# Propagations of two batches as seven block products, the layer norms' last step on ScalarE, and seven groups in flight, in a four-layer graph network

## The chip, the cores and the metric

The kernel runs on one core of a Trainium2 chip. Four engines compute: TensorE (PE, matrix products into PSUM; PEld is its loading of weights), VectorE (DVE), ScalarE (ACT) and GpSimd (POOL). SyncE (SP) issues the DMAs. Each engine works through its own queue in order; between engines there are semaphores. The metric is the device time of one execution in microseconds; lower is better. All numbers are float32.

## What is computed

x has 64 batches of 256 nodes with 128 features, adj is a 256x256 matrix. Four layers follow each other, each of them `x = layernorm(x + layer(x))`. A propagation is `adj @ x` for every batch.

```python
# layer 0: powers 1 to 3 of adj, the same adj twice, seven weights
parts = [x[..., None], chebyshev(adj, x, 3), chebyshev(adj, x, 3)]
y = einsum('bnik,iok->bno', concatenate(parts, axis=3), weight_1)
# layer 1
y = einsum('nm,bmo->bno', adj, einsum('bnf,fo->bno', x, weight)) + bias
# layer 2: normalised adjacency
A_norm = d[:, None] * (adj + eye) * d[None, :]
y = einsum('bnc,oc->bno', einsum('nm,bmc->bnc', A_norm, x), W) + b
# layer 3: five gated steps
m = einsum('nm,bmd->bnd', adj, h)
av = concatenate([m, m], axis=-1)
u3 = h @ u3_w.T + u3_b
z = sigmoid(av @ w3_w.T + w3_b + u3)
r = sigmoid(av @ w4_w.T + w4_b + u3)
hv = tanh(av @ w5_w.T + w5_b + (r * h @ u5_w.T + u5_b))
h = (1 - z) * h + z * hv
...
def layernorm(x, eps=1e-5):
    return (x - mean(x)) / sqrt(var(x) + eps)
```

## The kernel before

The 64 batches are cut into groups (line 644): 31 pairs and, at the end, two single batches (`ONES`, line 22). A group's tile has 128 partitions and 512 columns: two batches times two halves of the 256 nodes (T = 2) times 128 features. 256 nodes are therefore two 128-row blocks, and adj, held transposed in `aT`, is two by two blocks of 128x128. `a2T` is its square, `anT` the normalised matrix of layer 2, and `aTp` (lines 284 to 290) is `aT` with its rows spread for the layout that the steps of layer 3 use.

Group.record (line 532) writes down all work of one group. For layer 0: `transposes` or a transpose through DRAM (`tx`, `dx`, `xT`), the propagation `q` with `a2T`, products `first` and `second` (lines 564 and 577) into two banks `py`, and copies of these into `s0` by VectorE (line 583). Layers 1 and 2 (line 591): GpSimd adds the bias (`biased`, line 595), then come a propagation, a product with the weights and `residual`. Layer 3: five steps of a propagation `mg`, the gates `r`, `z`, `hv` on ScalarE (`gate_`), the products `pr` and `ph` with `w4T`, `w34T`, `w5T`, `u3T`, `u5T`, and on VectorE `rh`, `d`, `e` and `hT` (`tensor`, line 529). Between steps `packed` (line 500) turns the state on VectorE (`th`) and sends it through DRAM and back (`dh`, `h`); features of the two halves lie interleaved there, so that `pair_of` (line 370) reads every second element.

A propagation (line 457) is four products: for each of two batches, two halves kt as stationary operand (`lhsT`) against 256 columns of the matrix, added up in one PSUM bank `pm`. ScalarE copies the whole bank to `m` (`copied`, line 417).

A layer norm is `statistics` (line 422) and `normalise` (line 446). VectorE takes four bn_stats, four bn_aggr and an addition of eps (`ve`); GpSimd raises it to the power -0.5 (`rs`, line 438); VectorE then makes `y = (s - mean) * rs`, one tensor_scalar for each of four 128-column tiles (line 451).

No order is written by hand. Every operation is recorded with an engine, a cost, a lag and a rank in a Plan (line 50). Plan.order takes the engines' operations as they become ready in the plan's own time, the earliest start first and then the lowest rank, which is the oldest group; it gives out buffer slots of each kind (`slots`, line 199) on the way. The result is a fixed order for every engine's queue. At most `ACTIVE` = 6 groups are in flight: the first operation of a group waits in the plan for the last of the sixth before it (`gate`, line 652). In the last `LEVEL` = 6 groups the rank goes by progress, so that they end together. The last `END` = 8 batches turn the state back with TensorE (`pth`, line 640) and not through DRAM.

Of the kernel before, what the change touches and what calls it, by code (L numbers as in the profile page):

```python
# [8 lines left out]
F32 = mybir.dt.float32  # L9
# [4 lines left out]
P = 128  # L14
NB = 2
ACTIVE = 6
HEAD = 4
LEVEL = 6
# [3 lines left out]
ONES = (0, 2)  # L22
# [4 lines left out]
class Val:  # L27
# [3 lines left out]
    def __init__(self, kind, shape, name, nb=NB):  # L31
        self.kind, self.shape, self.name, self.nb = kind, shape, name, nb
        self.writer, self.readers, self.users = None, [], []
        self.slot = self.tile = None
# [15 lines left out]
class Plan:  # L50
# [9 lines left out]
    def add(self, engine, cost, lag, rank, run, reads=(), writes=(), after=()):  # L60
        if engine == "SP":
            lag += 700
        op = Op(len(self.ops), rank, engine, cost, lag, run, [*reads, *writes])
        op.deps.update(after)
        for v in reads:
            op.deps.add(v.writer)
            v.readers.append(op)
        for v in writes:
            if v.writer is not None:
                op.deps.add(v.writer)  # L70
            op.deps.update(v.readers)
            v.writer, v.readers = op, []
# [81 lines left out]
def kernel(  # L154
# [42 lines left out]
    SHAPES = {"bank": [P, 512], "x": [P, 512], "w": [P, 512], "st": [P, Q * 6], "mv": [P, Q * 2],  # L197
              "ve": [P, Q], "rs": [P, Q]}
    slots = {"bank": BANKS, "x": ACTIVE + 3, "w": 54, "dram1": 8, "dram2": 16, "st": 8, "mv": 8, "ve": 8, "rs": 8}
# [15 lines left out]
    def load(rank, name, shape, src):  # L215
        v = constant(name, shape)
# [20 lines left out]
    a_nat = load(-9, "a_nat", [P, T, N], adj.rearrange("(t p) m -> p t m", p=P))  # L237
# [55 lines left out]
    ahat, anT = constant("ahat", [P, T, N]), constant("anT", [P, T, N])  # L293
# [24 lines left out]


    w1s = load(1.3, "w1s", [P, C], w1)  # L320
    b1s = load(1.4, "b1s", [P, C], bass.AP(tensor=b1.tensor, offset=b1.offset, ap=[[0, P], [1, C]]))
    raw = {name: load(1.5, f"raw_{name}", [P, src.shape[1]], src)
           for name, src in (("w2", w2), ("w4", w4_w), ("w3", w3_w), ("w5", w5_w), ("u3", u3_w), ("u5", u5_w))}
    b2s = load(1.5, "b2s", [P, C], bass.AP(tensor=b2.tensor, offset=b2.offset, ap=[[0, P], [1, C]]))
    both = {name: constant(f"both_{name}", [P, C]) for name in ("w4", "w3", "w5", "w34")}
# [41 lines left out]
    def tile_of(v, q):  # L367
        return nat(v)[:, q, :]

    def pair_of(v, q):  # L370
        return v.ap.rearrange("p (b c t) -> p b t c", c=C, t=T)[:, q // T, q % T, :]
# [8 lines left out]
    class Group:  # L380
# [19 lines left out]
        def add(self, engine, cost, lag, run, reads=(), writes=()):  # L400
            after = () if self.first else self.gate
            self.count += 1
            op = plan.add(engine, cost, lag, self.rank(), run, reads, writes, after)
# [4 lines left out]
        def pe(self, cost, run, reads, writes):  # L408
            return self.add("PE", cost, 260, run, reads, writes)

        def dve(self, run, reads, writes, cost=None):
            return self.add("DVE", cost or dve_cost(self.width), 260, run, reads, writes)

        def act(self, run, reads, writes, cost=None):
            return self.add("ACT", cost or act_cost(self.width), 130, run, reads, writes)
# [6 lines left out]
        def statistics(self, tag, s):  # L422
            st, mv, ve, rs = (self.val(k, k + tag) for k in ("st", "mv", "ve", "rs"))
# [5 lines left out]
            def aggr():  # L429
                for q in range(self.q):  # L430
                    nc.vector.bn_aggr(mv.ap[:, 2 * q:2 * q + 2], st.ap[:, q * 6:(q + 1) * 6])  # L431
                nc.vector.tensor_scalar(ve.ap, mv.ap.rearrange("p (q k) -> p q k", k=2)[:, :, 1], EPS,  # L432
                                        None, op0=OP.add)

            self.dve(stats, [s], [st], 195 * self.q)
            self.dve(aggr, [st], [mv, ve], 67 * self.q + 142)
            self.add("POOL", 1010, 100,
                     lambda: nc.gpsimd.tensor_tensor(rs.ap, ve.ap, half[:, :self.q], op=OP.pow), [ve], [rs])  # L438
# [7 lines left out]
        def normalise(self, tag, s, mv, rs):  # L446
            y = self.val("w", "y" + tag)

            def run():
                for q in range(self.q):  # L450
                    nc.vector.tensor_scalar(nat(y)[:, q, :], nat(s)[:, q, :], mv.ap[:, 2 * q:2 * q + 1],  # L451
                                            rs.ap[:, q:q + 1], op0=OP.subtract, op1=OP.mult)

            self.dve(run, [s, mv, rs], [y], 257 * self.q)
# [245 lines left out]
```

## Time and profile before

| what | time |
|---|---|
| median of 3 runs (lowest to highest) | 1382.56 us (1382.29 to 1382.73) |
| the profiled execution | 1382.45 us |
| its span, first to last instruction | 1380.7 us |
| mean granted TensorE clock | 0.998 |
| PE: propagation products `pmg<-aTp,h` 128x256 | 1024 passes, 241.7 us |
| DVE: `y<-s,mv,rs` (line 451) | 512 instructions, 149.7 us |
| DVE: `rh<-r,hT`, 128x512 | 155 instructions, mean 725 ns |
| DVE: `s<-py` 128x256 (line 583) | 62 instructions, 25.1 us |
| ACT: `mg<-pmg`, 128x512 (line 419) | 155 instructions, mean 586 ns |
| POOL: `rs<-ve,half` (line 438) | 132 instructions, 137.9 us |
| POOL: `yb<-y,b2s` 128x512 (line 595) | 31 instructions, mean 1565 ns |

A row of the profile names line, engine, operation and the tiles that are written and read; "us" is busy time, a mean is that of one instruction. TensorE's float32 product shows as two instructions, called passes here. A busy TensorE says nothing of how fast it goes: passes overlap, and their pace is seen from the distance of their starts.

### The profile page before, as it was taken

To read this page: it belongs to the slowest core of one execution; us is meant where nothing else is said; L and a number is where in the kernel's file an instruction comes from. 1 tells how busy PE (TensorE), PEld (TensorE's weight loads), DVE (VectorE), ACT (ScalarE), POOL (GpSimd) and SP (SyncE) were. 2 spreads that over 40 slices of the span, in tenths; PEclk is the share of its full clock that TensorE was granted. 3 is DMA by queue.
4 is the path that set the end of the run, shared out by engine and by line. 5 is a ranking of instruction groups with operands and counts; after the bars stand their busy time and mean duration, and the time that the engine had idled before them with its cause. 6 is when DMAs were issued, how large, how long until landed. Compare 5 with 4: busy or idle time off the path is not lost.

```text
span 1380.7 us, 16602 instructions
## 1 busy us (share of the span) xinstructions
PE 1366.5 (99%) x5044; PEld 922.5 (67%) x5044; DVE 970.5 (70%) x2735; ACT 513.1 (37%) x833; POOL 236.1 (17%) x205
## 2 busy tenths in 40 slices
PE   9999999999999999999999999999999999999996
PEld 8866666666667766566676666667666677766664
DVE  4755686867667767776686767668685778875577
ACT  2233433333433233433424333442334332334443
POOL 1400021202111211011121211012221113210001
PEclk9999999999999999999999999999999999999999
DMA  6023233333333332343241334333232432233332
GB/s 177 31 77 91 85 115 115 91 98 105 112 107 90 109 92 75 97 137 110 64 137 54 108 108 117 95 92 106 78 107 84 118 97 85 85 92 90 86 103 65
DMA packets 271112, 134.08 MB, mean 97 GB/s; under 512 B 177584, under 2 KB 243632, under 8 KB 271024
## 3 DMA queue, kind: packets, MB, share of 16 engines
q1 hardware_dynamic: 271024, 133.03, 33.2%
q8 instruction: 40, 0.66, 0.2%
q14 instruction: 48, 0.39, 0.1%
HBM read 67.05 MB, written 65.54 MB: 96 GB/s over the span
## 4 chain that ended last, share of the span: by engine, by line
PE 97%; DVE 2%; DMA 0%; ACT 0%; issue 0%; POOL 0%; SPq 0%; POOLq 0%; DVEq 0%
PE pr L195 30%; PE ph L195 19%; PE pmg L195 19%; PE py L195 16%; PE pm L195 8%; PE pmq L195 4%; DVE y L451 1%; DMA h<-dh 0%; DVE st L427 0%; PE p_a L195 0%; PE warm L232 0%; DVE s L443 0%; DVE d L529 0%; DVE mv L431 0%; DVE e L529 0%
## 5 line engine op out<-in xcount | busy, mean ns | idle before, releaser
L195 PE MATMUL pr<-mg,w435u5T 128*128 128x512 f32 (+1 forms) x660 | 323.3, 580 | 1.7 <-ACT mg L419 1.4
L438 POOL TENSOR_TENSOR rs<-ve,half 128x4 f32<-128x4 f32 (+1 forms) x132 | 137.9, 1049 | 1049.8 <-DVE ve L432 1049.7
L529 DVE TENSOR_TENSOR d<-hv,hT 128x512 f32<-128x512 f32 (+1 forms) x165 | 113.6, 690 | 189.6 <-ACT hv L522 189.2
L195 PE MATMUL pmg<-aTp,h 128*128 128x256 f32 x1024 | 241.7, 379 | 0.4 <-DMA h<-dh 0.4
L195 PEld LDWEIGHTS pmg<-aTp,h 128*128 128x128 f32 x1024 | 200.4, 196 | 50.5 <-issue 24.4
L529 DVE TENSOR_TENSOR rh<-r,hT 128x512 f32<-128x512 f32 (+1 forms) x165 | 116.5, 706 | 128.2 <-ACT r L522 126.9
L195 PEld LDWEIGHTS pr<-mg,w435u5T 128*128 128x128 f32 x660 | 123.6, 190 | 101.0 <-issue 90.4
L419 ACT COPY mg<-pmg 128x512 f32<-128x512 f32 (+1 forms) x165 | 94.6, 573 | 257.0 <-PE pmg L195 236.5
L451 DVE TENSOR_SCALAR y<-s,mv,rs 128x128 f32<-128x128 f32 x512 | 149.7, 357 | 34.0 <-POOL rs L438 32.5
L195 PE MATMUL pr<-hT,w2u3T 128*128 128x512 f32 (+1 forms) x330 | 163.1, 580 | 1.1 <-DVE hT L529 1.1
L522 ACT ACTIVATE z<-pr,bsum 128x512 f32<-128x512 f32 (+1 forms) x165 | 111.3, 674 | 142.2 <-PE pr L195 137.4
L195 PE MATMUL ph<-mg,w435u5T 128*128 128x512 f32 (+1 forms) x330 | 163.4, 579 | 0.0
L195 PE MATMUL ph<-rh,w435u5T 128*128 128x512 f32 (+1 forms) x330 | 163.0, 579 | 0.0
L522 ACT ACTIVATE r<-pr,bsum 128x512 f32<-128x512 f32 (+1 forms) x165 | 111.3, 674 | 135.2 <-PE pr L195 132.7
L522 ACT ACTIVATE hv<-ph,bsum 128x512 f32<-128x512 f32 (+1 forms) x165 | 111.3, 674 | 53.0 <-PE ph L195 50.9
L529 DVE TENSOR_TENSOR e<-z,d 128x512 f32<-128x512 f32 (+1 forms) x165 | 113.8, 691 | 2.5
L529 DVE TENSOR_TENSOR hT<-hT,e 128x512 f32<-128x512 f32 (+1 forms) x165 | 113.1, 687 | 2.5
L427 DVE BATCH_NORM_STATS2 st<-s 128x6 f32<-128x128 f32 x512 | 109.7, 277 | 0.8
L195 PEld LDWEIGHTS ph<-rh,w435u5T 128*128 128x128 f32 x330 | 62.4, 190 | 69.3 <-issue 59.5
L195 PEld LDWEIGHTS ph<-mg,w435u5T 128*128 128x128 f32 x330 | 62.4, 190 | 67.5 <-issue 54.8
L504 DVE STREAM_TRANSPOSE th<-hT 128x512 f32<-128x512 f32 x132 | 91.0, 689 | 2.0
L195 PEld LDWEIGHTS pr<-hT,w2u3T 128*128 128x128 f32 x330 | 61.6, 190 | 42.0 <-issue 25.2
(79 smaller groups left out, 1373.7 us busy)
## 6 DMA issues: line engine op xcount, KB each, us to landing
dh<-th SPq DMA_DIRECT2D x155, 256.0 KB, 2.0
h<-dh SPq DMA_DIRECT2D x256, 128.0 KB, 2.5
x<-in_x_dram SPq DMA_DIRECT2D x31, 256.0 KB, 3.3
hT<-dh SPq DMA_DIRECT2D x124, 64.0 KB, 2.0
out_dram<-y SPq DMA_DIRECT2D x31, 256.0 KB, 2.4
xT<-dx SPq DMA_DIRECT2D x60, 128.0 KB, 2.5
dx<-tx SPq DMA_DIRECT2D x29, 256.0 KB, 2.6
dn<-tn SPq DMA_DIRECT2D x28, 256.0 KB, 2.0
```

The source lines that it names most:

```text
L195: nc.tensor.matmul(o, lhsT, rhs, start=start, stop=stop, skip_group_check=shared)
L419: self.act(lambda: nc.scalar.copy(t.ap, ps.ap), [ps], [t])
L427: nc.vector.bn_stats(st.ap[:, q * 6:(q + 1) * 6], nat(s)[:, q, :])
L438: lambda: nc.gpsimd.tensor_tensor(rs.ap, ve.ap, half[:, :self.q], op=OP.pow), [ve], [rs])
L451: nc.vector.tensor_scalar(nat(y)[:, q, :], nat(s)[:, q, :], mv.ap[:, 2 * q:2 * q + 1], rs.ap[:, q:q + 1], op0=OP.subtract, op1=OP.mult)
L504: self.dve(lambda: nc.vector.transpose(turn.ap.rearrange("p (u j t) -> p u t j", t=T, j=32), src.ap.rearrange("p (u t i) -> p u t i", t=T, ...
L522: self.act(lambda: nc.scalar.activation(t.ap, ps.ap, func, bias=bias[1], scale=1.0), [ps, bias[0]], [t], act_cost(self.width) + 100)
L529: self.dve(lambda: nc.vector.tensor_tensor(out(t), way(a), way(b), op=op), [a, b], [t])
```

## The change

A pair's propagation is a product of a 2x2 block matrix (batch by half) with the 2x2 blocks of the adjacency. It is computed with seven block products and additions around them (Strassen's scheme in Winograd's form) instead of eight. `seven` records: GpSimd makes four blocks of differences of the state's blocks in three instructions (`ts`, `tq`); TensorE multiplies in four visits (`first`, `middle`, `more`, `rest`), each product 128 columns wide, into the four 128-column parts of one bank; ScalarE keeps the first product before the second is added to it (`kept`), and later copies out the first output block; VectorE adds the others together (`post1`, `post2`) and writes `m`. Sums of the adjacency's blocks are made once on VectorE (`block_sums`). The first two groups (start below HEAD) keep the old form for `q`, since `near` is passed on as `fast=not near`; everything else, 254 propagations, takes the new one.

Further: `statistics` also makes the negated mean (`nm`) and GpSimd multiplies it with `rs`, so that `normalise` is an ACTIVATE with scale and bias on ScalarE; the copies into `s0` go to ScalarE; ACTIVE and LEVEL are 7; ONES is (0, 0), so all 32 groups are pairs. Some buffers grow, and loaded raw weights take slots instead of constants. The plan learns of several writers of one buffer (`joint`).

```diff
-ACTIVE = 6
+ACTIVE = 7
 HEAD = 4
-LEVEL = 6
+LEVEL = 7
 END = 8
 STEPS = 5
 WARM = 12
-ONES = (0, 2)
+ONES = (0, 0)
...
         for v in writes:
-            if v.writer is not None:
-                op.deps.add(v.writer)
             op.deps.update(v.readers)
-            v.writer, v.readers = op, []
+            if not joint:
+                op.deps.update(v.writers)
+                v.writers = []
+            v.writers.append(op)
+            v.readers = []
...
-    slots = {"bank": BANKS, "x": ACTIVE + 3, "w": 54, "dram1": 8, "dram2": 16, "st": 8, "mv": 8, "ve": 8, "rs": 8}
+    slots = {"bank": BANKS, "x": ACTIVE + 3, "w": 60, "th": 8, "q": 4, "dram1": 8, "dram2": 16, "st": 12, "mv": 12, "ve": 24, "rs": 12}
...
+    def block_sums(rank, name, aTs):
+        v = constant(f"s_{name}", [P, 5, P])
+        a11, a12, a21, a22 = (aTs.ap[:, kt, t * P:(t + 1) * P] for t in range(T) for kt in range(T))
+        def run():
+            nc.vector.tensor_add(v.ap[:, 0, :], a21, a22)
+            nc.vector.tensor_sub(v.ap[:, 1, :], v.ap[:, 0, :], a11)
+            nc.vector.tensor_sub(v.ap[:, 2, :], a11, a21)
+            nc.vector.tensor_sub(v.ap[:, 3, :], a12, v.ap[:, 1, :])
+            nc.vector.tensor_scalar(v.ap[:, 4, :], a22, -1.0, None, op0=OP.mult)
+        pre(rank, "DVE", 1200, run, [aTs], [v])
+        sums_of[aTs] = v
+    block_sums(0.6, "aT", aT)
+    block_sums(0.6, "a2T", a2T)
+    block_sums(0.6, "anT", anT)
+    block_sums(0.7, "aTp", aTp)
...
-    def tile_of(v, q):
-        return nat(v)[:, q, :]
-
-    def pair_of(v, q):
-        return v.ap.rearrange("p (b c t) -> p b t c", c=C, t=T)[:, q // T, q % T, :]
+    def tiles(v):
+        return v.ap.rearrange("p (b t c) -> p b t c", t=T, c=C)
+    def pairs(v):
+        return v.ap.rearrange("p (b c t) -> p b t c", c=C, t=T)
...
-            st, mv, ve, rs = (self.val(k, k + tag) for k in ("st", "mv", "ve", "rs"))
+            st, mv, ve, rs, nm = (self.val(k, n + tag) for k, n in (
+                ("st", "st"), ("mv", "mv"), ("ve", "ve"), ("rs", "rs"), ("ve", "nm")))
             def stats():
                 for q in range(self.q):
@@ -429,13 +456,17 @@
             def aggr():
                 for q in range(self.q):
                     nc.vector.bn_aggr(mv.ap[:, 2 * q:2 * q + 2], st.ap[:, q * 6:(q + 1) * 6])
-                nc.vector.tensor_scalar(ve.ap, mv.ap.rearrange("p (q k) -> p q k", k=2)[:, :, 1], EPS,
-                                        None, op0=OP.add)
+                mean, var = (mv.ap.rearrange("p (q k) -> p k q", k=2)[:, k] for k in range(2))
+                nc.vector.tensor_scalar(ve.ap, var, EPS, None, op0=OP.add)
+                nc.vector.tensor_scalar(nm.ap, mean, -1.0, None, op0=OP.mult)
+            def scales():
+                nc.gpsimd.tensor_tensor(rs.ap, ve.ap, half[:, :self.q], op=OP.pow)
+                nc.gpsimd.tensor_tensor(mv.ap[:, :self.q], nm.ap, rs.ap, op=OP.mult)
             self.dve(stats, [s], [st], 195 * self.q)
-            self.dve(aggr, [st], [mv, ve], 67 * self.q + 142)
-            self.add("POOL", 1010, 100,
-                     lambda: nc.gpsimd.tensor_tensor(rs.ap, ve.ap, half[:, :self.q], op=OP.pow), [ve], [rs])
+            self.dve(aggr, [st], [mv, ve, nm], 67 * self.q + 240)
+            self.add("POOL", 1300, 100, scales, [ve, nm], [rs, mv])
...
-                    nc.vector.tensor_scalar(nat(y)[:, q, :], nat(s)[:, q, :], mv.ap[:, 2 * q:2 * q + 1],
-                                            rs.ap[:, q:q + 1], op0=OP.subtract, op1=OP.mult)
-
-            self.dve(run, [s, mv, rs], [y], 257 * self.q)
+                    nc.scalar.activation(nat(y)[:, q, :], nat(s)[:, q, :], AF.Identity, bias=mv.ap[:, q:q + 1],
+                                         scale=rs.ap[:, q:q + 1])
+            self.act(run, [s, mv, rs], [y], 370 * self.q)
...
-        def propagate(self, tag, h, aTs, ins=None, outs=None):
-
-            ps = self.val("bank", "pm" + tag)
+        def propagate(self, tag, h, aTs, ins=None, blocks=False, fast=True):
+            if fast and self.nb == 2:
+                return self.seven(tag, h, aTs, ins or tiles, blocks)
+            ps, outs = self.val("bank", "pm" + tag), by_block if blocks else None
             def run():
-                o, a = (outs or plain)(ps), ins or tile_of
+                o, a = (outs or plain)(ps), ins or tiles
                 for b in range(self.nb):
                     for kt in range(T):
-                        mm(o[b], a(h, b * T + kt), aTs.ap[:, kt, :], kt == 0, kt == T - 1)
+                        mm(o[b], a(h)[:, b, kt], aTs.ap[:, kt, :], kt == 0, kt == T - 1)
             self.pe(pe_cost(N, self.q), run, [h, aTs], [ps])
             return self.copied("m" + tag, ps)
+        def seven(self, tag, h, aTs, ins, blocks):
+            sums = sums_of[aTs]
+            ps, m = self.val("bank", "pm" + tag), self.val("w", "m" + tag)
+            ts, tq, u = self.val("th", "ts" + tag), self.val("q", "tq" + tag), self.val("th", "us" + tag)
+            def row(v, k):
+                return v.ap[:, k * P:(k + 1) * P]
+            def o(v, q, blocks=blocks):
+                if blocks:
+                    return v.ap.rearrange("p (k q i) -> p q k i", k=4, i=32)[:, q]
+                return v.ap.rearrange("p (q k i) -> p q k i", k=4, i=32)[:, q]
+            def ts01():
+                nc.gpsimd.tensor_tensor(ts.ap[:, :2 * P].rearrange("p (x c) -> p x c", x=2), ins(h)[:, 1], ins(h)[:, :, 0],
+                                        op=OP.subtract)
+            def ts2():
+                nc.gpsimd.tensor_tensor(row(ts, 2), ins(h)[:, 1, 1], row(ts, 0), op=OP.subtract)
+            def ts3():
+                nc.gpsimd.tensor_tensor(tq.ap, row(ts, 2), ins(h)[:, 0, 1], op=OP.subtract)
+            def block(q, w, a, start=False):
+                mm(row(ps, q), w, a, start, True, shared=True)
+            def first():
+                block(0, ins(h)[:, 0, 0], aTs.ap[:, 0, :P], True)
+            def middle():
+                block(2, row(ts, 0), sums.ap[:, 0, :])
+                block(1, row(ts, 1), sums.ap[:, 2, :])
+                block(3, row(ts, 2), sums.ap[:, 1, :])
+            def more():
+                block(0, ins(h)[:, 0, 1], aTs.ap[:, 1, :P])
+            def rest():
+                block(2, ins(h)[:, 1, 1], sums.ap[:, 3, :])
+                block(1, tq.ap, sums.ap[:, 4, :])
+            def post1():
+                nc.vector.tensor_tensor(row(u, 0), row(u, 1), row(ps, 3), op=OP.add)
+                nc.vector.tensor_tensor(row(u, 2), row(u, 0), row(ps, 1), op=OP.add)
+                nc.vector.tensor_tensor(o(m, 3), o(u, 2, False), o(ps, 2, False), op=OP.add)
+            def post2():
+                both = o(u, 0, False)[:, None].to_broadcast([P, 2, 4, 32])
+                nc.vector.tensor_tensor(o(m, slice(1, 3)), o(ps, slice(1, 3), False), both, op=OP.add)
+            started = self.pe(pe_cost(P, 1), first, [h, aTs], [ps])
+            kept = self.act(lambda: nc.scalar.copy(row(u, 1), row(ps, 0)), [ps], [u], act_cost(P))
+            self.add("POOL", 700, 100, ts01, [h], [ts])
+            self.add("POOL", 400, 100, ts2, [h, ts], [ts])
+            self.add("POOL", 400, 100, ts3, [h, ts], [tq])
+            self.pe(pe_cost(P, 3), middle, [ts, sums], [ps], True, (started,))
+            self.pe(pe_cost(P, 1), more, [h, aTs], [ps], True, (kept,))
+            self.dve(post1, [ps, u], [u, m], 690)
+            self.act(lambda: nc.scalar.copy(o(m, 0), o(ps, 0, False)), [ps], [m], act_cost(P), True)
+            self.pe(pe_cost(P, 2), rest, [h, tq, sums], [ps], True)
+            self.dve(post2, [ps, u], [m], 340, True)
+            return m
...
-            qT = self.propagate("q", x_, a2T)
+            qT = self.propagate("q", x_, a2T, fast=not near)
...
-                    nc.vector.tensor_copy(nat(s0).rearrange("p (b t) c -> p t b c", t=T)[:, t],
+                    nc.scalar.copy(nat(s0).rearrange("p (b t) c -> p t b c", t=T)[:, t],
...
-                self.dve(summed, [py[t]], [s0], dve_cost(self.nb * C))
+                self.act(summed, [py[t]], [s0], act_cost(self.nb * C))
...
-                m = self.propagate(f"g{s}", h, ats, ins, by_block)
+                m = self.propagate(f"g{s}", h, ats, ins, True)
...
```

## The prediction

> **What bounds the kernel now.** I read the page's shares first, then the chain of waits, then the engines' busy time by stretches of the span, then what TensorE waited for.
>
> ```profile
> PE 1366.5 (99%) x5044; PEld 922.5 (67%) x5044; DVE 970.5 (70%) x2735; ACT 513.1 (37%) x833; POOL 236.1 (17%) x205
> ...
> PE 97%; DVE 2%; DMA 0%; ACT 0%; issue 0%; POOL 0%; SPq 0%; POOLq 0%; DVEq 0%
> ...
> 60.00:1340.00 1280.00, 1278.99 (x4652) 852.63 (x4651) 903.63 (x2492) 484.41 (x778) 214.17 (x179) 1.00 0.33 97
> 1340.00:1381.00 41.00, 29.55 (x113) 19.16 (x111) 30.85 (x99) 14.11 (x27) 4.83 (x6) 0.93 0.24 68
> ...
> PE pth L475 <- DVE hT L529: 2.6, 1, 2.6
> PE pr L195 <- ACT mg L419: 1.4, 3, 0.5
> ```
>
> The stretch rows give the length, then the busy time of PE, PEld, DVE, ACT and POOL. From 60 to 1340 us TensorE stands still for 1 us in all; nearly all its idle time lies in the last 41 us, where 29.55 are busy, and at the start. TensorE's own instructions are the time; nothing else is late. So the first question is what they cost per pass, and the second whether the other engines can still feed it.
>
> A float32 product is two passes. Their spacing is read from starts in the timeline:
>
> ```profile
> 700.17 1.89 PE L195 MATMUL pm<-aT,y 128*128 128x256 f32 x8
> ...
> 701.90 1.89 PE L195 MATMUL pmg<-aTp,h 128*128 128x256 f32 x8
> ...
> 703.63 1.05 PE L195 MATMUL py<-w1s,m 128*128 128x128 f32 x8
> ...
> 704.52 1.02 PE L195 MATMUL pr<-hT,w2u3T 128*128 128x512 f32 x2
> 705.38 1.02 PE L195 MATMUL pr<-mg,w435u5T 128*128 128x512 f32 x2
> ```
>
> A propagation is 8 passes of 256 columns: 1.73 us, 0.216 each. Eight passes of 128 columns, each with new weights, take 0.89 us: 0.112 each. So narrow passes run at the rate of their columns, although a weight load lasts 0.19 us in the rows.
>
> **What the Trainium skill says.** "SBUF — State Buffer", section "Who interferes with whom": a VectorE instruction with two SBUF inputs and a GpSimd instruction that reads SBUF exclude each other for their whole length; with one SBUF input outside the two-port modes there is no conflict. The trace agrees:
>
> ```profile
> 710.04 1.65 POOL L595 TENSOR_TENSOR yb<-y,b2s 128x512 f32<-128x512 f32 x1 [1.23 <-DVE y L451]
> ...
> 709.88 0.68 DVE L529 TENSOR_TENSOR rh<-r,hT 128x512 f32<-128x512 f32 x1
> 710.59 1.65 DVE L529 TENSOR_TENSOR d<-hv,hT 128x512 f32<-128x512 f32 x1
> ```
>
> yb waits for rh and takes 1.65 instead of 1.27; d then waits for yb and takes 1.65 instead of 0.69. The PSUM-reading s<-py,yb never exceeds 0.692. "GPSIMD Engine Reference", section "Elementwise — side-by-side cycle accounting": about 2.6 cycles per element with two inputs. The trace: 1.27 us for 512 columns (median), 0.726 for 256 (shortest), so 2.1 ns a column and 0.45 us for 128. "ScalarE: Activation LUTs", section "What ACT_TABLE_LOAD costs": 186 ns + 0.833 per element, 93 more for each pointer operand, neighbours overlapping by 93. ACTIVATE with one pointer on 256 columns measured 474 against the page's 493, so I use it: 128 columns with two pointers 0.48, spaced 0.39 (an estimate; the trace has no such instruction).
>
> **The change part by part.**
> *Products.* 14 passes of 128 columns (1.57) replace 8 of 256 (1.73): -0.16 us. 32 groups times 8 propagations, less two for q of the first two groups: 254 x 0.16 = **-40.6 us**, all on the path. Pairs instead of single batches at the end leave the columns as they were.
>
> *VectorE.* Gone: y 149.7, the s copies of line 583 26. New for each propagation: three 128-column adds and one of 256, one input in PSUM. Nearest rows: the s copy from PSUM on 128 columns 0.285, s<-py,yb on 256 0.418; 3 x 0.285 + 0.418 = 1.27, x 254 = 323, some 25 less where neighbours overlap: 298. nm adds 128 x 0.175 = 22, at most. Lock: in before the four groups rh, d, e, hT (means 725, 707, 709, 704 ns on 512 columns) average 26 ns over the undisturbed 0.685 (the median of s<-py,yb is 683), 16 us in 620, beside 81 us of yb. After, GpSimd's pieces are more but shorter; a wait grows with the sum of squared lengths: 254 x (0.726² + 2 x 0.454²) + 64 x 1.27² = 341 against 103 before, so 3.3 x 16 = 53, 37 more. Sum: 970.5 - 149.7 - 26 + 298 + 22 + 37 = 1152, or **86%** of some 1340: still under TensorE, but no longer far.
>
> *GpSimd.* 0.726 + 2 x 0.454 = 1.63 for each propagation, 415 us; 128 tiny products between 0.1 (its memsets) and 1.0 (its pow), I take 0.2: 26. Sum 677, **50%**.
>
> *ScalarE.* The 128x512 copies go (-150), two of 128 columns come (254 x 2 x 0.266 = 135), y comes (512 x 0.39 = 200), s copies 64 x 0.373 = 24: 722, 54%. Hidden unless a queue forms; it costs nothing here.
>
> *New waits.* Each propagation now visits TensorE four times. Behind a waiting product stands every later product of all groups, so what matters is how much TensorE work the new order places into each gap. I summed that from the instruction order of the changed program with the passes priced above, outside the first 60 and last 50 us, against what the handoff needs (0.2 us from a product's end to a reader, as ACT m at 702.10 after pm; 0.06 back). From the three middle products to the last two (post1 lies between, 0.86 + 0.26 = 1.1): median 3.7, one in twenty below 1.54. From the last product to the first use of m (post2, 0.68): 2.4 and 1.08. From the first product to the second into the same block (a copy, 0.52): 3.2 and 0.87. From the start of GpSimd's differences to their product (0.726 + 0.454 + 0.1 = 1.28): 4.8 and 1.94. In some 1,200 handoffs the shortfalls add up to 3 us. Before, the least margin was 0.87 (1.71 for a copy that needs 0.84); now the thinnest twentieth has 0.35 to 0.66. VectorE queues at 86% and lock waits of up to 1 us will break part of these: 60 thin handoffs x 0.1 = **+6**, bounds 2 and 30.
>
> *GpSimd held off.* A run of VectorE instructions with two SBUF inputs can keep it out: the longest yb took 4.66 us. With 826 such GpSimd instructions against 64, I take 1 propagation in 20 late by 0.5 us beyond its margin: 13 x 0.5 = **+6**, bounds 0 and 30.
>
> *Start.* All groups are then in the layers that load GpSimd most; in the new order its instructions sum to 88% and 104% of TensorE's 20th-40th and 40th-60th us of work (before: 15.7 in 20-60). Twenty VectorE instructions for the block sums (20 x 0.29 = 5.8) lie in the first 20 us, where it was busy 6.55. **+4**, bounds 0 and 10.
>
> *End.* The last group is a pair: from its fourth d to the end I add 2.8 (d, e, hT, th), 4.3 (two DMAs), 4.4 (differences, products, adds), 9.1 (products, gates, d, e, hT, transposes), 3.1 (s, statistics), 4.8 (pow, product, y), 2.4 (store) less overlaps of 4: 27 us, with 14 us of TensorE work left. Before it was 23.5 (1357.19 to 1380.7) with 10.8 left. About **+3**, bounds -2 and +8. Seven groups in flight instead of six is what pays the longer chain of a group: 7 x 42 us may pass between its gate and its end.
>
> *DMAs.* None is added; SP's queue loses the single batches' issues.
>
> **Sum.** 1380.7 - 40.6 + 6 + 6 + 4 + 3 = 1359.1 span. The profiled run took 1382.45, 1.75 over its span, and the median is 1382.56: **1361 us**.
>
> **Rivals.**
> *TensorE starves on the lock (slower).* Place: GpSimd's differences and VectorE's d, e, hT, which now compete in every step. The point from which it decides: more than 43 us of new TensorE idle time, that is 0.17 us for each propagation. That comes if not 11% (53 of 496 us) but half of GpSimd's SBUF-reading time blocks VectorE: 1152 - 53 + 248 = 1347 busy, the longer queue, and TensorE waits in turn, about 1347 + 20 at the start + 30 in handoffs = 1397. For it: one d of 1.65, one yb of 4.66. Against it: in before VectorE lost only 16 us to 81 of yb (20%), and that with pieces three times as long.
> *GpSimd slower than extrapolated.* The four 256-column yb average 0.887; then 128 columns cost 0.58, a propagation 2.05, GpSimd sums to 783 (58%) and the first 60 us overflow: +8 there, +8 in late differences: 1377. For it: inputs in strides of two elements for the packed h, which no row shows. Against: those averages hold lock waits with y, which leaves VectorE.
> *Narrow passes fall to the weight load's pace.* 14 x 0.19 = 2.66 for a propagation: +236 us. Against it: the 0.112 measured with new weights for each; not believed.
> *Nothing gets worse:* idle time as in before, 1382.5 - 40.6 = 1342.
>
> **How the numbers follow.** My case, with its neighbours down to 1342: 0.69. GpSimd slower: 0.15, two thirds of it still faster. Lock, slower: 0.15. Weight pace: 0.01. A difference below 0.2% (2.8 us) can't be told from none. Faster 0.79, same 0.04, slower 0.17. The range leaves out 0.04 below and about 0.16 above: 1342 to 1384; the likeliest case alone has 1342 to 1374.
>
> **What would show it.** Products into pm, pmg, pmq: 14 passes at about 0.112. Busy PE near 1322 to 1335. DVE near 85%, POOL near 50%, ACT near 54%. rh, d, e, hT on average 0.75 to 0.80 instead of 0.71. In the stretch from 60 to 1340 TensorE idle for about 12 us, most of it before products that read ts. It would be wrong if PE waits <- POOL or <- DVE summed to over 40 us, or if the passes were spaced 0.13 and more.

## The result, and the profile after

The changed kernel takes **1423.55 us** (median of 4 runs, 1422.73 to 1424.55) against 1382.64 us for the kernel before on the same chip: 1.0296 times as long, 95% interval 1.0278 to 1.0314. The forecast was 1361.

The page of the changed kernel, first the shares of the engines, then the chain of work that ended last:

```profile
PE 1364.6 (96%) x6510; PEld 930.2 (65%) x6510; DVE 1141.0 (80%) x3288; ACT 683.1 (48%) x1638; POOL 754.5 (53%) x1089
...
PE 57%; DVE 18%; ACT 4%; issue 4%; POOL 3%; DMA 1%; DVEq 0%; SPq 0%; ACTq 0%; POOLq 0%
```

No engine is full any more. The chain, 97% TensorE in the kernel before, now runs through TensorE for 57% and through VectorE for 18%. The stretches of the span (length, then busy PE, PEld, DVE, ACT, POOL; the last three columns are the granted clock, the DMA share and GB/s) say where:

```profile
60.00:1340.00 1280.00, 1246.40 (x5957) 846.15 (x5956) 1044.20 (x2972) 621.76 (x1493) 694.67 (x994) 1.00 0.33 94
1340.00:1421.00 81.00, 63.70 (x227) 34.64 (x225) 61.76 (x167) 35.63 (x75) 25.39 (x35) 0.91 0.28 82
```

TensorE, which stood still for 1 us between 60 and 1340 us, now does so for 33.6, and that is not all: a pass that waits for its weights counts as busy. If the excess of each distance between starts over the pace of its width (0.112, 0.216, 0.4295 us) is added up, TensorE loses some 90 us in the whole span, though it is idle for only 56 of them; before it lost 14. That is +76. In all, 361 distances are too long by more than 0.05 us (51 before). Its own work falls by nearly what was forecast: the 3,556 narrow passes, at their 112.4 ns where nothing interrupts them, are worth 399.7 us, in place of 438.9 for 2,032 wide ones: -39. No single wait explains the 76; the largest rows of what TensorE waited for (us in total, times, longest) are

```profile
PE ph L198 <- DVE rh L629: 4.6, 9, 0.8
PE pmg L198 <- POOL tsg L525: 4.4, 5, 2.0
PE pth L575 <- DVE hT L629: 4.3, 1, 4.3
PE pm L198 <- DVE m L551: 3.4, 4, 1.2
```

and, of the weight loads alone (without the rows "issue", in which the engine waited for nothing that the profile shows),

```profile
PEld ph L198 <- DVE rh L629: 25.9, 52, 1.5
PEld pr L198 <- DVE mg L555: 11.6, 31, 0.9
PEld pmg L198 <- ACT mg L565: 10.1, 18, 1.3
```

A weight load may run ahead of its product (the loads are busy for 930 us beside 1365 us of products, in a span of 1421), so not each of its waits costs time. The rows and the 361 distances show that the loss is spread over hundreds of short waits, in all parts of a group. Two places in the trace show how one comes about. The first, on VectorE and then on TensorE (start, length, what is written and read, instructions):

```profile
1112.93 1.62 DVE L454 BATCH_NORM_STATS2 st<-s 128x6 f32<-128x128 f32 x8
1114.47 0.27 DVE L549 TENSOR_TENSOR us<-us,pm 128x128 f32<-128x128 f32 x1
1114.77 0.29 DVE L550 TENSOR_TENSOR us<-us,pm 128x128 f32<-128x128 f32 x1
1115.10 0.29 DVE L551 TENSOR_TENSOR m<-us,pm 128x128 f32<-128x128 f32 x1
...
1116.41 0.28 DVE L549 TENSOR_TENSOR us<-us,pm 128x128 f32<-128x128 f32 x1
1116.73 0.29 DVE L550 TENSOR_TENSOR us<-us,pm 128x128 f32<-128x128 f32 x1
1117.05 0.29 DVE L551 TENSOR_TENSOR m<-us,pm 128x128 f32<-128x128 f32 x1
```

```profile
1115.44 0.49 PE L198 MATMUL pm<-s_anT,y 128*128 128x128 f32 x2 [0.66 <-DVE m L551]
1115.76 0.39 PE L198 MATMUL pm<-s_anT,tq 128*128 128x128 f32 x2
1117.39 0.49 PE L198 MATMUL pm<-s_aT,y 128*128 128x128 f32 x2 [1.24 <-DVE m L551]
```

Two propagations wait for their three adds (`post1`) before the last two products (`rest`). The adds take 0.9 us, but stand behind two statistics runs (1.62 us) and the aggregates between 1115.4 and 1116.4. In these two gaps it is VectorE's queue that holds TensorE up, more than the adds themselves. What such gaps make of the whole loss, only the experiments can say. The second place is GpSimd's queue:

```profile
973.10 1.18 POOL L521 TENSOR_TENSOR ts<-y 128x256 f32<-128x256 f32 x1
974.36 0.46 POOL L525 TENSOR_TENSOR ts<-y,ts 128x128 f32<-128x128 f32 x1
974.78 1.01 POOL L464 TENSOR_TENSOR rs<-ve,half 128x4 f32<-128x4 f32 x1
...
976.02 0.73 POOL L521 TENSOR_TENSOR tsg<-h 128x256 f32<-128x256 f32 x1
976.71 0.91 POOL L528 TENSOR_TENSOR tq<-ts,y 128x128 f32<-128x128 f32 x1
977.57 0.46 POOL L525 TENSOR_TENSOR tsg<-h,tsg 128x128 f32<-128x128 f32 x1
```

```profile
976.27 1.03 DVE L629 TENSOR_TENSOR e<-z,d 128x512 f32<-128x512 f32 x1
```

```profile
974.79 0.83 PE L198 MATMUL pm<-s_anT,ts 128*128 128x128 f32 x6
975.46 0.40 PE L198 MATMUL pmg<-aTp,h 128*128 128x128 f32 x2
975.70 0.39 PE L198 MATMUL pmq<-a2T,x 128*128 128x128 f32 x2
978.04 0.68 PE L198 MATMUL pmg<-s_aTp,tsg 128*128 128x128 f32 x4 [1.96 <-POOL tsg L525]
```

VectorE's e reads two inputs from SBUF beside GpSimd's differences; e takes 1.03 us and tq 0.91, twice the 0.46 of the piece after it. TensorE waits 1.96 us for the difference that starts at 977.57. (The rows of TensorE also show the pace: six narrow passes from 974.79 to 975.46, 0.112 each.)

### The profile page after: what moved, and what is told of

The parts are those of the page before. It is cut to its first block, busy times and chain, and to the rows that moved or that the text cites. A ratio compares the mean times of both kernels' runs of the same rounds, so it can differ in the third digit from the quotient of the medians.

```text
span 1420.8 us, 22283 instructions
## 1 busy us (share of the span) xinstructions
PE 1364.6 (96%) x6510; PEld 930.2 (65%) x6510; DVE 1141.0 (80%) x3288; ACT 683.1 (48%) x1638; POOL 754.5 (53%) x1089
## 4 chain that ended last, share of the span: by engine, by line
PE 57%; DVE 18%; ACT 4%; issue 4%; POOL 3%; DMA 1%; DVEq 0%; SPq 0%; ACTq 0%; POOLq 0%
PE pr L198 19%; PE ph L198 13%; PE pmg L198 12%; PE py L198 9%; PE pm L198 3%; DVE st L454 2%; DVE hT L629 2%; DVE e L629 2%; ACT y L482 2%; DVE d L629 2%; DVE s L474 1%; DVE rh L629 1%; PE pmq L198 1%; ACT hv L622 1%; DVE th L604 1%
## 5 line engine op out<-in xcount | busy, mean ns | idle before, releaser
L198 PE MATMUL pr<-mg,w435u5T 128*128 128x512 f32 x640 | 324.2, 597 | 2.9 <-ACT r L622 1.6
L464 POOL TENSOR_TENSOR rs<-ve,half 128x4 f32<-128x4 f32 x128 | 144.3, 1127 | 276.2 <-DVE nm L461 274.5
L482 ACT ACTIVATE y<-s,mv,rs 128x128 f32<-128x128 f32 x512 | 210.4, 483 | 73.7 <-POOL mv L465 71.2
L629 DVE TENSOR_TENSOR d<-hv,hT 128x512 f32<-128x512 f32 x160 | 124.0, 777 | 86.8 <-ACT hv L622 86.4
L198 PE MATMUL ph<-rh,w435u5T 128*128 128x512 f32 x320 | 164.9, 600 | 4.8 <-DVE rh L629 4.6
L198 PE MATMUL pr<-hT,w2u3T 128*128 128x512 f32 x320 | 164.9, 600 | 4.1 <-DVE hT L629 2.3
L198 PE MATMUL ph<-mg,w435u5T 128*128 128x512 f32 x320 | 163.3, 593 | 0.0
L629 DVE TENSOR_TENSOR rh<-r,hT 128x512 f32<-128x512 f32 x160 | 122.0, 764 | 42.8 <-ACT r L622 41.1
L629 DVE TENSOR_TENSOR hT<-hT,e 128x512 f32<-128x512 f32 x160 | 124.9, 784 | 1.2
L629 DVE TENSOR_TENSOR e<-z,d 128x512 f32<-128x512 f32 x160 | 123.1, 771 | 1.4
```

Source lines behind the costliest of these rows:

```text
L198: nc.tensor.matmul(o, lhsT, rhs, start=start, stop=stop, skip_group_check=shared)
L482: nc.scalar.activation(nat(y)[:, q, :], nat(s)[:, q, :], AF.Identity, bias=mv.ap[:, q:q + 1], scale=rs.ap[:, q:q + 1])
L629: self.dve(lambda: nc.vector.tensor_tensor(out(t), way(a), way(b), op=op), [a, b], [t])
```

## The experiments

Times are medians; the kernel before took 1382.2 to 1382.6 each time that it ran beside these kernels. Several kernels leave work out, which is said with each.

**Which part of the change costs?** Eight products everywhere, the rest of the change kept:

```diff
-            if fast and self.nb == 2:
+            if False:
```

> Every propagation as the eight products of before; ScalarE's layer norm step, seven groups in flight and pairs alone stay. TensorE's own work is then 1360 us again. If the seven products with what they need around them cause the new idle time (all theories below), some 20 us of idle time are left: 1375 to 1385 us. If the norm on ScalarE or the seven groups in flight cause it, 1400 us or more.

Measured 1387.73 (ratio 1.0039, 1.0024 to 1.0054). TensorE is busy for 1279.93 of the 1280 us from 60 to 1340. So the norm step on ScalarE, seven groups and pairs cost 5 us together, and in the trace these lie at the end: 16.5 us idle after 1340, against 11.2 before. The propagations cost the rest.

**GpSimd's differences left out** (the products read the state's blocks instead):

```diff
-            self.add("POOL", 700, 100, ts01, [h], [ts])
...
-            self.pe(pe_cost(P, 3), middle, [ts, sums], [ps], True, (started,))
+            self.pe(pe_cost(P, 3), middle, [h, sums], [ps], True, (started,))
```

> Seven products, but GpSimd's differences are left out: TensorE reads the state's blocks in their place, so the result is another one. TensorE's work stays 1321 us. Lock theory (GpSimd and VectorE exclude each other[...], the delays become TensorE's): nearly all new idle time goes, 1345 to 1360 us. Order theory (the planner's lengths for VectorE's additions and the rest are too short, so the order leaves too little room): only the part with GpSimd goes, about 1385 us. Load theory (VectorE at 80% with two more handoffs for each propagation is enough): 1395 to 1410 us.

Measured 1392.53, in none of the three ranges: 31 us of the loss go with GpSimd's differences, but seven products without them are still not faster than eight.

**GpSimd busy and late, without reading SBUF** (memsets of 739 and twice 466 ns, and every wait on them, stand in for the differences):

```diff
-                nc.gpsimd.tensor_tensor(row(ts, 2), ins(h)[:, 1, 1], row(ts, 0), op=OP.subtract)
+                nc.gpsimd.memset(ts.ap[:, :440], 0.25)
```

> Each of GpSimd's differences is replaced by a memset of about its length (768 and 440 columns for 0.73 and 0.45 us), which reads nothing from SBUF; the products read what it wrote, so all waits stay, and the result is another one. Lock theory: as without the differences or a little more, 1350 to 1370 us, and rh, d, e, hT back to 0.71 us. Order and load theories: no change, 1405 to 1425 us.

Measured 1393.79, again between the ranges. GpSimd is busy for 654 us (754 with the differences) and TensorE still waits for it, and yet 30 us are regained: reading SBUF beside VectorE costs these. Against no differences at all the kernel is 1 us slower, but that is not the price of waiting for GpSimd. Without differences, 1,024 more passes take the packed state itself as stationary operand, and such passes follow each other more slowly (shown under "One visit"), which costs some 6 us. So the waits for GpSimd cost some 7 us (both are estimates). One row of each kernel shows the lock at work, first changed, then memsets:

```profile
L629 DVE TENSOR_TENSOR e<-z,d 128x512 f32<-128x512 f32 x160 | 123.1, 771 | 1.4
```

```profile
L628 DVE TENSOR_TENSOR e<-z,d 128x512 f32<-128x512 f32 x160 | 109.9, 689 | 1.4
```

**Is it the lock?** z, hv and e are written in place into their PSUM banks, so that d, e and hT read only one input from SBUF:

```diff
-            t = self.val("w", name)
+            t = ps if keep else self.val("w", name)
...
-                e = self.tensor(f"e{s}", OP.mult, z, d)
+                e = self.tensor(f"e{s}", OP.mult, z, d, into=z)
```

> The changed kernel (1423.6 us) with z, hv and e written in place into their PSUM banks, so that d, e and hT read one input from PSUM and only rh reads two from SBUF. Theory of the lock (30 us of the loss): three of four locked instructions go, so 1398 to 1408, VectorE's busy time some 40 us less, d, e and hT near 690 ns on average. Rival (the loss is in the handoffs and their order, and lock waits only ride on them): within 6 us of 1423.6. A third, that banks held longer stop TensorE: 1430 or more, with waits of pr and ph on VectorE.

Measured 1395.57: 28 us regained, a little more than expected. (ScalarE's two gates into PSUM are also 26 ns shorter, 659 instead of 685; no run separates their share.) Of the four rows only rh, which still reads two tiles of SBUF, stays long:

```profile
L629 DVE TENSOR_TENSOR rh<-r,hT 128x512 f32<-128x512 f32 x160 | 123.5, 773 | 51.4 <-ACT r L622 51.0
L629 DVE TENSOR_TENSOR pr<-pr,d 128x512 f32<-128x512 f32 x160 | 110.0, 690 | 1.1
L629 DVE TENSOR_TENSOR d<-ph,hT 128x512 f32<-128x512 f32 x160 | 109.4, 684 | 109.2 <-ACT ph L622 108.8
L629 DVE TENSOR_TENSOR hT<-hT,pr 128x512 f32<-128x512 f32 x160 | 108.0, 677 | 1.1
```

That is the rule of the Trainium skill ("SBUF — State Buffer", "Who interferes with whom") read the other way round: a VectorE instruction with at most one SBUF input, outside its two-port modes, does not contend with GpSimd. The trace agrees, with 684 ns for d instead of 777.

**Lengths in the plan.** The planner is told what the trace of the changed kernel shows (differences 830, 600 and 570 ns, adds 850 and 380, two-input adds 720, others alike):

```diff
-            self.add("POOL", 700, 100, ts01, [h], [ts])
+            self.add("POOL", 830, 100, ts01, [h], [ts])
```

> The changed kernel with the planner told the lengths of its own profile: differences 830, 600 and 570 ns, the adds 850 and 380, two-input adds of VectorE 720, the norm step 400 a tile, the scales 1420. Same instructions in another order. Order theory: the idle time falls by half or more, under 1385 us. Lock and load theories: 1405 to 1425 us.

Measured 1406.48, within the range of the lock and load theories. Still, with the lock in place, a better guess of lengths is worth 17 us. The same without differences (two-input adds at 640):

> Without GpSimd's differences, with the planner told the measured lengths of the adds (850, 380), of VectorE's two-input adds (640), of the norm step (400 a tile) and of the scales (1420). Order theory: 1370 us or less, from 1392.5. Load and round-trip theories: 1380 to 1395 us.

Measured 1388.18, 4 us better than 1392.53. Without the lock, the order is not what is wrong, so far as lengths go.

**VectorE's load.** Without differences, and three of four bn_stats left out:

```diff
-                for q in range(self.q):
-                    nc.vector.bn_stats(st.ap[:, q * 6:(q + 1) * 6], nat(s)[:, q, :])
+                nc.vector.bn_stats(st.ap[:, :6], nat(s)[:, 0, :])
```

> Without GpSimd's differences as in the run before (1392.5 us, 1321 of it TensorE's work, some 45 us of new idle time left), and of each layer norm's four bn_stats three are left out, the planner told so: 77 us of VectorE's work less, 1087 to about 1010 us, 73% of the span, with every product, copy and addition around the seven products as it was. The result is another one. Load theory (VectorE's queue is too full): most of the 45 us goes, 1350 to 1365 us. Round-trip theory (each propagation makes TensorE wait for ScalarE and VectorE between its four visits, whatever VectorE's load): 1380 us or more.

Measured 1387.84: 4.7 us. As long as the waits of the visits stand, load alone brings little.

**ScalarE's queue.** Without differences, the norm step given to the planner as four operations, so that copies can go between its pieces:

```diff
-            self.act(run, [s, mv, rs], [y], 370 * self.q)
+                self.act(run, [s, mv, rs], [y], 370, q > 0)
```

> The kernel without GpSimd's differences (1392.5 us), with the layer norm's last step given to the planner as four ScalarE instructions of 370 ns instead of one run of 1480, so that copies can go between them. Theory of ScalarE's queue (copies that release products wait behind that run): 1375 to 1385. Rival (VectorE's runs or the number of handoffs): within 4 us of 1392.5.

Measured 1395.49, 3 us worse. This theory falls.

**One visit.** Without differences, all seven products in one operation, one ScalarE copy after them; VectorE's adds and the two small copies are left out:

```diff
+            self.pe(pe_cost(P, 7), whole, [h, aTs, sums], [ps])
+            self.act(lambda: nc.scalar.copy(m.ap, ps.ap), [ps], [m])
```

> The kernel without GpSimd's differences (1392.5 us), with all seven products of a propagation in one visit of TensorE and one ScalarE copy of the whole bank after them; VectorE's adds and the two small copies are left out, so the output differs. Theory of the visits (the 40 us of mid-span stalls come from leaving and re-entering a propagation three times): the stalls go, and the time is that of eight products with the rest of the change, 1387.7, less 39 us of products: 1346 to 1355, TensorE idle from 60 to 1340 us under 8 us. Rival (the stalls belong to the narrow passes themselves, or to the seven groups' order): 1375 or more, TensorE idle over 25 us in the middle.

Measured 1356.78, 2 us above the range. From 60 to 1300 us TensorE is not idle at all (columns as above):

```profile
60.00:1300.00 1240.00, 1240.00 (x6027) 856.51 (x6026) 754.65 (x2049) 663.24 (x1273) 227.53 (x286) 1.00 0.34 99
```

So seven products are worth 31 us here (1387.73 to 1356.78), where nothing stalls, and splitting the propagation into visits, with the copies and adds between them, takes 36 away. That includes VectorE's load, whose busy time is 815 us here and 1087 with the adds.

Why 31 and not 39: in this run the propagations' passes follow at 114.5 ns on average, about half of them at 116 to 118. The trace shows which:

```profile
700.33 0.83 PE L198 MATMUL pm<-s_anT,y 128*128 128x128 f32 x6
701.00 0.39 PE L198 MATMUL pm<-anT,y 128*128 128x128 f32 x2
...
703.61 0.87 PE L198 MATMUL pmg<-s_aTp,h 128*128 128x128 f32 x6
704.32 0.40 PE L198 MATMUL pmg<-aTp,h 128*128 128x128 f32 x2
```

Six passes with `y` as stationary operand take 0.67 us, six with the packed state `h`, which is read at every second element, 0.71. All 1,024 distances within `pmg<-s_aTp,h` in this run are over 115 ns (mean 117.8), all within `pm<-s_anT,y` under it (mean 111.7). It isn't the other operand: in the changed kernel, `pmg<-s_aTp,tsg`, where GpSimd's differences stand in place of `h`, has a mean of 111.4. That kernel has 768 passes with the packed state, this one and the other kernels without differences have 1,792. They pay 1,024 times 6.1 ns, some 6 us (an estimate), for it.

**The second copy.** The last two products do not need ScalarE's copy of block 0 (`m0`), but the plan and the buffer's waits have them behind it. Without differences, the copy is recorded after them:

```diff
-            self.act(lambda: nc.scalar.copy(o(m, 0), o(ps, 0, False)), [ps], [m], act_cost(P), True)
             self.pe(pe_cost(P, 2), rest, [h, sums], [ps], True)
+            self.act(lambda: nc.scalar.copy(o(m, 0), o(ps, 0, False)), [ps], [m], act_cost(P), True)
```

> The kernel without GpSimd's differences (1392.5 us), with ScalarE's second copy (block 0 into m) recorded behind the last two products instead of ahead of them; output as in that kernel. Theory of ScalarE's copies (the last two products wait for a copy that they do not need): 1373 to 1383, and the waits of pm and pmg on ACT mg are gone. Rival (VectorE's three adds come last anyway): within 4 us of 1392.5.

Measured 1384.41: 8 us, a little short of the range, but the wait was real.

**The three adds.** On top of that, `post1` too is recorded behind the last two products; it then reads blocks that already hold them:

> The kernel without GpSimd's differences and with ScalarE's second copy late (1384.4 us), with VectorE's three adds too recorded behind the last two products; they then read blocks that already hold those products, so the output differs. All work and all instructions stay, only the wait of the last two products for the adds goes. Theory of the wait (28 us lie in handoffs from VectorE back to TensorE): 1358 to 1370. Rival (VectorE's load, 80% instead of 60%, makes other products wait): 1378 or more.

Measured 1379.97: 4.4 us more, the rival's side. TensorE no longer waits for the adds between visits, and 23 us are still missing to the one visit. With three of four bn_stats left out of this kernel:

> The kernel without differences and with the second copy and the three adds late (1380.0 us), with three of the four pieces of each statistics run left out (77 us of VectorE, which falls from 79% to some 74%); output differs. If what is left over one visit (23 us) is VectorE's queue: 1363 to 1371. If it is the first copy, the longer chain or the ends: 1376 or more.

Measured 1370.39. The same 77 us of VectorE's work that brought 4.7 under the old waits bring 9.6 here. VectorE's queue is part of it; 13.6 us between this kernel and the one visit stay open. Two candidates are untested. No run takes away the handoff of the first copy (`kept`), for which the weight loads of the steps' propagations wait 53 times in this kernel, 21.2 us in all; and a PSUM bank is held through all four visits.

**Half the propagations.** Seven products in q, layers 1 and 2 and the first step only (126 of 254), or in the last four steps only (128):

```diff
-                m = self.propagate(f"g{s}", h, ats, ins, True)
+                m = self.propagate(f"g{s}", h, ats, ins, True, s > 0)
```

> Seven products only in the propagations of layers 0 to 2 and of the first step of layer 3 (126 of 254); the last four steps have eight. TensorE's work 1340 us. If idle time comes from VectorE's load and the lock, it grows faster than the number of sevens: 10 us of it instead of 74, so 1385 - 20 + 10 = 1375 us. If it is a fixed sum for each propagation (0.3 us), 1385 - 20 + 37 = 1402 us.

> Seven products only in the last four steps of layer 3 (128 of 254). TensorE's work 1340 us. As with the other half: 1375 us if the idle time comes from load and lock, 1402 us if it is a fixed sum for each propagation. A difference between the halves shows where a round trip hurts: here the state comes through DRAM first and the gates follow at once.

Measured 1399.53 and 1385.14, the first near the fixed sum's 1402, the second between the two forecasts: nearly the same number of products saved, 14 us apart. In the layers seven products cost 12 us against eight everywhere, in the steps they bring 2.6. In the layers VectorE also has its statistics and GpSimd its powers and biases, which may be the reason; no run separates it.

**Mended.** PSUM gates, late copy, measured lengths and single batches at the end, in all propagations; then in the last four steps alone; then in all with 500 ns more lag for the first copy and both sets of adds; at last that in all five steps:

```diff
-            self.dve(post1, [ps, u], [u, m], 850)
+            self.dve(post1, [ps, u], [u, m], 850, lag=760)
```

> The changed kernel with z, hv and e in PSUM (alone 1395.6), the second copy late (alone 8 us), the planner told measured lengths, and two single batches at the end as in the kernel before (the pairs cost about 5). Output as before. If these causes add up: 1395.6 - 8 - 5 - 0 to 4 = 1378 to 1384, no difference from the kernel before that matters. If the parts overlap (each mends the same stalls): 1386 to 1393.

> The same with seven products in the last four steps alone (128 of 254 propagations; unmended 1385.1). Products give 20 us against eight everywhere; if the visits' stalls come from VectorE's and ScalarE's queues and so grow faster than their number, half the propagations have less than half the stalls: 1366 to 1374, faster than the kernel before. If stalls go with the number of visits: 1377 to 1382.

> The mended kernel with 500 ns more given to the planner for the handoffs of the first copy and of both sets of adds, so that it puts other groups' products in between. Theory that the order leaves the handoffs too little room: 8 to 20 us faster than the mended kernel without it. Rival (the wait is VectorE's queue, which shifts with the products): within 4 us, or slower as groups take longer.

> The mended kernel with room in the plan, with seven products in all five steps (160 of 254 propagations), eight in q, 1 and 2. Against the mended half (1373.1) it saves 32 times 0.16, 5 us, of products. If the stalls stay as small as there (1 us from 60 to 1340): 1367 to 1370. If first steps, whose differences come when the layers' statistics fill VectorE and GpSimd, bring stalls of more than 0.16 us each: 1374 or more.

Measured, in this order: 1391.30, **1373.12**, 1382.44 and 1375.50. The causes don't add up in all propagations (4 us where some 13 were to be had). Room in the plan brings 9 us, so there the order does leave the handoffs too little. In the last four steps alone (124 propagations here, as the single batches keep four products), the mended kernel beats both: 0.9931 of the kernel before (0.9919 to 0.9944). What seven products have in these 9 us isn't measured, since no run has eight products with the same mends. By the count of distances used above TensorE loses some 20 us in the whole span, and its stretch row is nearly without idle time again:

```profile
60.00:1340.00 1280.00, 1278.88 (x5457) 869.34 (x5456) 908.71 (x2589) 659.81 (x1441) 431.32 (x667) 1.00 0.34 98
```

With a fifth step the kernel is 2.4 us slower, though 5 us of products are saved. That run also has the room in its plan, so the step's stalls and the room aren't separated.

## Why the prediction was wrong

**The failed step** is "New waits", +6, and with it "GpSimd held off", +6: together 12 us of new idle time, bounds 2 to 60. By the times it is 67: 36 for the visits with their copies and adds (one visit against four) and 31 for the differences. As the runs without differences have slower products, the second is some 6 more, so 73 in all, against the 76 counted in the trace.

The step priced each handoff by itself: 1.1 us needed between the middle products and the last two, a median of 3.7 us of TensorE work in between, so only the thin twentieth could fail. It named VectorE's queue at 86% and the lock as what would break some handoffs, but priced that at 60 times 0.1 us. The reader doesn't start when the product ends; it starts when its engine has worked off what stands in front. At 1112.93 that was 1.62 us of bn_stats, more than the whole handoff. The step also missed that the last two products wait for `m0`.

The experiments split the 36 so: 8 for the wait on `m0`, 4 for the wait on the three adds, 10 that go with 77 us of VectorE's statistics once those waits are gone, and 14 that stay open. So the queue in front of the reader is shown as a part, and not as the whole.

**Products, -40.6.** Right in pace: 112.4 ns in the changed kernel, -39 us. It is less, 31 us, in the one-visit run, where all products of the last four steps read the packed state itself; the forecast's 0.112 came from passes that don't.

**VectorE, GpSimd, ScalarE.** 1152, 677 and 722 us forecast, 1141, 754 and 683 measured. GpSimd came close to its rival's 783: a propagation's differences take 0.81 + 0.60 + 0.57 = 1.98 us with lock waits, and 0.75 + 0.52 + 0.49 = 1.76 with PSUM gates, where 1.63 was extrapolated. The memset run (1.67 us for a propagation) shows that GpSimd's work costs some 7 us by the estimate above as long as it reads no SBUF. The norm step's piece with two pointers measures 483 ns, against the estimate of 0.48 from the Trainium skill ("ScalarE: Activation LUTs", "What ACT_TABLE_LOAD costs").

**The lock.** Its size was right and its price wrong. rh, d, e and hT were forecast at 0.75 to 0.80 and measure 0.764 to 0.784; over 640 instructions that is 57 us beyond 0.685, 41 more than before, where the formula said 37. But the working booked these on VectorE's sum, under cover, and so at nothing; taking the lock away regains 28 to 30 us. So the cover, TensorE's other work, wasn't there. These 28 to 30 us overlap with what the plan can win: measured lengths brought 17 us with the lock and 4 without differences. A likely reason, argued and not shown by a run, is that d, e and hT stand in the same queue ahead of the adds that TensorE waits for.

**Start, +4, and End, +3.** TensorE's busy time in the first 60 us fell from 57.96 to 54.53: 3.4. The end cost about 5, by the run with eight products.

**The rival** "TensorE starves on the lock" had the right sign, threshold (43 us of new idle time; it is 76) and half of the place, at a chance of 0.15. Its mechanism was wrong: it needed VectorE nearly full at 1347 us. VectorE is at 80%, and TensorE starves all the same.

**The sign of being wrong**, waits of PE on POOL and DVE of over 40 us, did not show: these rows sum to 27 us (5 before), while the kernel lost 76: the wait of a weight load hides in a pass that counts as busy.

## What to carry to other kernels

When an operation that ran through in one visit is cut into dependent visits, price each handoff with the reader's queue: the runs that can stand ahead of it, and not its own duration alone. Count every buffer wait that the split brings, needed or not. An engine that is busy for 80% can still hold up the one that bounds the kernel, if the second waits for the first within every unit of work. Such a trick may pay in part of the loop: here in the last four steps, and not in the layers.

## What was not expected of the hardware

- Lock waits of 0.09 us on average (777 instead of 684 ns for d) cost 28 us of the kernel's time, although VectorE was at 80%: without those of d, e and hT VectorE's busy time fell by 48 us (1141.0 to 1092.6) and GpSimd's by 85 (754.5 to 669.5).
- ScalarE is quicker with a gate in PSUM: 659 and 658 ns for z and hv in place, 685 into SBUF. The Trainium skill ("ScalarE: Activation LUTs", "Step-by-step: what each stage is for") says so without a number. VectorE's e, written to PSUM, took 690 ns.
- Narrow float32 passes have two paces: about 112 ns, and 116 to 118 where the stationary operand is read at every second element (117.8 against 111.7 in the one-visit run). No run here says why the stride costs 6 ns.
